# Keys and values of seven tile pairs by seven half-size products for eight, weights through the piece ring

## The chip, the cores and the metric

The kernel runs on one core of one Trainium2 chip. The metric is the device time of one execution in microseconds; lower is better. The core has five engines with queues of their own: TensorE (PE, with its weight loads listed as PEld), VectorE (DVE), ScalarE (ACT), GpSimd (POOL) and SyncE (SP), which here issues all transfers. All data is float32.

## The reference

An attention layer and a LoRA mixture-of-experts layer, each between layer norms and with a residual sum, on 4 sequences of 512 tokens of 1024 features:

```python
# attention: 32 query heads, 8 key/value heads, 32 features each
qkv = x @ w_qkv.T + b_qkv
q, k, v = jnp.split(qkv, [q_dim, q_dim + kv_dim], axis=-1)
...
q = apply_rope(q, 0)
k = apply_rope(k, 0)
...
scores = jnp.einsum('bhqd,bhkd->bhqk', q, k) / math.sqrt(HEAD_DIM)
scores = jnp.where(causal[None, None, :, :], scores, jnp.float32(-1e+20))
attn = jax.nn.softmax(scores, axis=-1)
...
return out @ w_o.T + b_o

# mixture of experts: 8 experts of rank 16, the best 2 of each token
gate_logits = jnp.einsum('bsd,ed->bse', x, gate_w)
...
result = jnp.einsum('bsd,od->bso', x, base_w) + base_b
...
return result + SCALING * lora_out

# around them
x = x + _layernorm(attention(_layernorm(x)))
x = x + _layernorm(experts(_layernorm(x)))
```

The change concerns the product that gives keys and values: 1024 input features by 512 outputs (256 of keys, 256 of values) for every token.

## The kernel before

**Tiles.** The 2048 tokens are 16 tiles of 128, four to a sequence. A tile is loaded (`load_x`, tile `xa`, one buffer), normed and transposed into `xnT` (`normed_x`; two buffers, named `T_xn` in the profile). From it come keys and values (`keys_values`) and queries (`queries`), then attention in groups of heads (`scores`, `turn`, `values`, giving `aT`), the output product (`attention_out`, `acc_o`), norms, the gate (`gated`, `acc_gl`) and the base product of the experts (`ffn`, `acc_f`).

**Products.** A plain product of a tile by 512 columns of weights is eight products of 128 features, summed in one PSUM bank (`project`, L618). `whole` does that with plain weights. `seven` computes a 2 by 2 block product, two tiles by the two halves of the 1024 outputs, with the features also in two halves, by seven half-depth block products for eight (Strassen's method in Winograd's form): each block is four products of 128 features by 512 columns. It needs four sums and differences of the two tiles' transposed inputs (`s1` to `s4`, tag `part`, four buffers in `part_slots`) and, for four of the seven blocks, sums and differences of the weights' quarters. Each block's bank is added by DVE onto earlier ones (`take`, L727), and two combinations of results follow at the blocks 4 and 5 (`combine`, L343, on DVE or POOL, whichever the planner finds sooner). Queries, output and base products of tile pairs go through `seven`; only the first pair's queries and the last pair's output do not.

**Mixed weights.** The sums of weights are made once by `mix`: for a chunk it loads two tiles of 128 rows by 1024 columns (L423, 512 KB each, `wide` tiles, four buffers in `w_slots`), combines their halves in four steps on DVE or POOL and stores both back to DRAM as `mixed_q`, `mixed_o` or `mixed_f` (L438). Two chains run side by side, each with two chunks of q and then two of o; when both are done (`has_w`), four chunks of f follow one by one. `attended` gives the first pair's output tiles (`w`, also `wide`) only after `has_w`.

**The piece ring.** The weights of `whole` and `seven` are streamed in pieces of 128 by 512 (256 KB) by `bring_pieces` (L489), in the order in which the main lane uses them, through a ring of 13 buffers. A piece of a mixed weight waits for its chunk. All transfers stand in SyncE's one queue, in order.

**Keys and values before.** `w_qkv`'s 512 key/value columns are loaded into SBUF at the start (`wkv_sb`, eight transfers of 256 KB, 16 KB of each partition) and stay there. For each tile `keys_values` does eight products of 512 columns (`acc_kv`), then DVE adds the bias to the values (L938) and the keys (L948), the keys are turned (`rotate`) and transposed (`turn_k`).

**The order.** `Order` is a planner that runs while the program is built. It holds costs of every operation (`Op`, `Step`), tracks which buffers and data are free and due, and writes each engine's instructions out in the order in which it would start them. For TensorE it has lanes: scores first, then transposes, values, and the dense lanes `gl_lane`, `kv_lane` and `main_lane`, of which the first with a ready step is taken, a started accumulation going on first. The main lane's own order is fixed: queries of pair 0 and 1; then for each pair n its output, the queries of pair n+2 and its base products. The last pairs' blocks are interleaved by hand. A sequence's last tile comes before its first in the last sequence (tokens 13, 14, 15, 12), so the pairs 6 and 7 of the attention are (13, 14) and (15, 12), while keys and values are made in the order of the tokens, and tile 12's input is normed a second time for its queries (`T_xn_12q`).

Of the kernel before, what the change touches and what calls it, by code (L numbers as in the profile page):

```python
# [11 lines left out]
F32 = mybir.dt.float32  # L12
# [4 lines left out]
P = 128  # L17
# [248 lines left out]
def kernel(  # L266
# [27 lines left out]
    BANKS, SOFT, RING = 4, 8, 13  # L294
# [44 lines left out]
    def combine(urgent, out, in0, in1, op, engines=("dve", "pool")):  # L339


        def issue(engine):
            engine.tensor_tensor(out=out(), in0=in0(), in1=in1(), op=op)  # L343

        on = {"dve": (0.85, partial(issue, nc.vector)), "pool": (1.3, partial(issue, nc.gpsimd))}
        return Op(urgent, **{e: on[e] for e in engines})
# [21 lines left out]
    wkv_sb = const.tile([P, ND, 2 * KVD], F32, name="wkv_sb")  # L368
# [15 lines left out]
    def loads(what):  # L384
# [13 lines left out]
    plain = {"q": w_qkv, "o": w_o, "f": w_base}  # L398
    mixed = {name: dram.tile([D, D], F32, name=f"mixed_{name}") for name in plain}
    has_mixed = {(name, c): Task() for name in plain for c in range(ND // 2)}  # L400
    biases = {
        "q": bqkv_sb,
# [3 lines left out]
    bias_steps = {name: const.tile([P, 512], F32, name=f"bias_step_{name}") for name in plain}  # L406
    has_bias = {name: Task() for name in plain}

    def mix(chunks):

        lo, hi = slice(0, 512), slice(512, D)
        for name, c in chunks:
            w = plain[name]
            a_rows, b_rows = (slice((k + c) * P, (k + c + 1) * P) for k in (0, ND // 2))
            pair = []
            for rows in (a_rows, b_rows):
                yield w_slots.take()

                def bring():
# [3 lines left out]
                    nc.sync.dma_start(out=pair[-1], in_=w[rows, :D])  # L423

                yield sp(P * D * 4 / 1024 / RATE, bring, 1)
            yield LANDS
            a, b = pair
            for out, in0, in1 in (
# [5 lines left out]
                yield combine(2, lambda: out, lambda: in0, lambda: in1, ALU.subtract)  # L434
            for rows, t in ((a_rows, a), (b_rows, b)):
                yield sp(
                    P * D * 4 / 1024 / RATE,
                    lambda: nc.sync.dma_start(out=mixed[name][rows, :], in_=t),  # L438
# [7 lines left out]
    def bias_step(name):  # L446
        yield loaded["b", name]
        b = biases[name]
        yield combine(
            4, lambda: bias_steps[name], lambda: b[:, 512:D], lambda: b[:, :512], ALU.subtract  # L450
# [16 lines left out]
    def block(name, of, h, k, uses=1):  # L467

        new = []
        for c in range(ND // 2):  # L470
            at = (h * ND // 2 + c) * P
            after = has_mixed[name, c] if of is mixed else Task(0.0)
            new.append(Piece(of[name][at : at + P, k * 512 : (k + 1) * 512], after, uses))
        return new

    def bring_pieces():
# [5 lines left out]
        pieces = dict.fromkeys(step.piece for step in main_lane if step.piece is not None)  # L482
        for k, piece in enumerate(list(pieces)):
            yield piece.after
            yield piece_slots.take()

            def issue():
                piece.sb = weights.tile([P, 512], F32, tag="piece", name=f"piece_{k}")
# [119 lines left out]
    def project(lhsT, w, n, name, needs, take):  # L608
# [15 lines left out]
        for c in range(len(needs)):  # L624
            us = 0.858 if n == 512 else 0.24
# [1128 lines left out]
```

## Time and profile before

| | |
|---|---|
| runs | 1163.82 us median of 3 (1163.1 to 1165.35) |
| the profiled execution | span 1162.7 us from first to last instruction; granted clock 0.996 in the mean |
| key/value products, `acc_kv` L618 | 256 matmuls for 128 products, 119.4 us busy, median 592 ns of one |
| additions behind them, L938 and L948 | 16 each of 128x256 on DVE, 418 and 402 ns |
| product with 136 columns, `acc_gl` | 256 matmuls, 34.0 us busy, mean 280 ns |
| `combine` on 128x512, L343 | 859 ns on DVE (`w<-w,w`), 1309 ns on POOL (`y<-y,w`) |
| weight load of a product | 190 ns, on PEld beside the matmuls |
| mixing transfers | q: 512 KB, 6.6 us to landing; back 7.3 us |
| tile transfers | `xa` 256 KB, 3.8 us to landing; output 256 KB, 3.9 us |
| all DMA | 231.48 MB, mean 199 GB/s |

A float32 product appears as two matmuls and two weight loads. Matmuls are pipelined: one lasts longer than the distance to the next, so the length of a run of them, less one duration, divided by one less than their number gives the spacing. The page's time from issue to landing is a median.

### The profile page before, as it was taken

Reading aid. Unit: us, or ns where it says so; the run is one execution under the profiler, and the core shown is the slowest. Engines: PE = TensorE matmul, PEld = TensorE weight load, DVE = VectorE, ACT = ScalarE, POOL = GpSimd, SP = SyncE. Lnnn points to the kernel's source line nnn. Section 1 sums busy time; section 2 is a strip of 40 time slices with the busy share of each in tenths; the row PEclk is TensorE's granted clock in tenths of the full one; section 3 lists DMA queues with packets and bytes.
Section 4 is the critical chain, followed back from the end, with each engine's and each line's share of the span. In section 5 each row is a group of like instructions: output and inputs, shape, how many; then the busy total and the mean of one; then the engine's idle time right before and its main releaser. Section 6 shows DMA issues by size and latency. Waiting matters only on the chain.

```text
span 1162.7 us, 21371 instructions
## 1 busy us (share of the span) xinstructions
PE 1136.4 (98%) x7240; PEld 624.5 (54%) x7240; DVE 832.6 (72%) x1629; ACT 530.1 (46%) x1545; POOL 611.7 (53%) x859
## 2 busy tenths in 40 slices
PE   7999999999999999999999999999999999999997
PEld 3455554655556455565555555456555555556443
DVE  4787767987678756787667876768866787668564
ACT  0354554555555355555434434455644555454010
POOL 2686856743756435544555253654545564547231
PEclk9999999999999999999999999999999999999999
DMA  9879777563773637625477443673457745585783
GB/s 349 277 255 310 248 253 263 170 220 97 257 239 96 199 109 253 192 83 176 141 244 256 137 135 118 219 229 106 149 168 233 243 135 160 164 268 187 221 285 118
DMA packets 117740, 231.48 MB, mean 199 GB/s; under 512 B 13440, under 2 KB 14464, under 8 KB 117632
## 3 DMA queue, kind: packets, MB, share of 16 engines
q1 hardware_dynamic: 117632, 230.12, 60.7%
q8 instruction: 58, 0.95, 0.3%
q14 instruction: 50, 0.41, 0.1%
HBM read 209.09 MB, written 20.97 MB: 198 GB/s over the span
## 4 chain that ended last, share of the span: by engine, by line
PE 86%; DVE 7%; DMA 3%; POOL 1%; ACT 1%; issue 1%; SPq 0%; POOLq 0%; ACTq 0%
PE acc_f L618 18%; PE acc_o L618 16%; PE acc_q L618 14%; PE pt_p L1485 11%; PE acc_kv L618 8%; PE sc L1390 7%; PE av L1508 6%; PE acc_gl L618 2%; DVE nmax L1469 2%; PE pt_xn L593 1%; PE pt_h L593 1%; DMA piece<-in_w_qkv_dram 1%; ACT pr L1411 1%; PE pt_q L1010 1%; DMA xa<-in_x_dram 1%
## 5 line engine op out<-in xcount | busy, mean ns | idle before, releaser
L1425 POOL TENSOR_SCALAR pr<-pr,rtot 128x256 f32<-128x256 f32 (+3 forms) x512 | 300.5, 602 | 251.9 <-DVE rtot L1440 183.3
L1411 ACT ACTIVATE pr<-sc,nmax 128x256 f32<-128x256 f32 (+3 forms) x512 | 265.0, 536 | 121.8 <-DVE nmax L1469 63.6
L1469 DVE TENSOR_REDUCE nmax<-sc 128x2 f32<-128x768 f32 (+3 forms) x176 | 198.2, 1126 | 33.7 <-ACT pr L1411 30.6
L1485 PEld LDWEIGHTS pt_p<-ident,pr 128*128 128x128 f32 x1280 | 144.5, 141 | 59.3 <-issue 49.1
L1485 PE MATMUL pt_p<-ident,pr 128*128 128x128 f32 x1280 | 173.2, 276 | 2.4 <-DVE raw_q L727 1.0
L335 ACT COPY prT<-pt_p 128x512 f32<-128x512 f32 (+1 forms) x261 | 134.1, 548 | 62.4 <-PE pt_p L1485 61.0
L1459 DVE TENSOR_TENSOR sc<-sc,cmask 128x256 f32<-128x256 f32 (+2 forms) x176 | 96.7, 550 | 48.6 <-PE sc L1390 39.0
L335 ACT COPY aT<-av 128x128 f32<-128x128 f32 (+2 forms) x83 | 26.1, 315 | 222.1 <-PE av L1508 222.0
L618 PE MATMUL acc_f<-piece,s_f 128*128 128x512 f32 x256 | 120.1, 602 | 2.1 <-DVE s_f L343 2.1
L618 PE MATMUL acc_kv<-wkv_sb,T_xn 128*128 128x512 f32 x256 | 119.4, 597 | 0.0
L1411 ACT ACTIVATION_READ_ACCUMULATOR pr<-sc,nmax 128x1 f32 x512 | 108.3, 212 | 0.0
L618 PE MATMUL acc_o<-piece,aT 128*128 128x512 f32 x232 | 105.9, 594 | 0.0
L618 PE MATMUL acc_q<-piece,s_q 128*128 128x512 f32 x224 | 105.4, 595 | 0.1
L618 PE MATMUL acc_q<-piece,T_xn 128*128 128x512 f32 x224 | 103.9, 594 | 0.1
L618 PE MATMUL acc_o<-piece,s_o 128*128 128x512 f32 x224 | 102.8, 593 | 0.0
L1390 PE MATMUL sc<-kT,qT 32*128 32x384 f32 (+3 forms) x1024 | 93.9, 464 | 0.5 <-ACT pr L1411 0.5
L1508 PEld LDWEIGHTS av<-prT,v 128*32 128x32 f32 x2560 | 64.8, 109 | 50.1 <-issue 35.0
L618 PE MATMUL acc_f<-piece,T_h 128*128 128x512 f32 x192 | 90.0, 592 | 0.0
L343 POOL TENSOR_TENSOR y<-y,w 128x512 f32<-128x512 f32 x61 | 79.1, 1309 | 20.3 <-ACT w L568 14.9
L1508 PE MATMUL av<-prT,v 128*32 128x128 f32 x2560 | 88.7, 276 | 0.2 <-DVE prT L336 0.2
L336 DVE COPY prT<-pt_p 128x512 f32<-128x512 f32 (+1 forms) x91 | 58.3, 642 | 31.3 <-PE pt_p L1485 29.7
L541 POOL TENSOR_TENSOR rstd<-veps,neg_half 128x1 f32<-128x1 f32 x64 | 35.0, 549 | 86.1 <-DVE veps L537 85.8
(154 smaller groups left out, 1416.3 us busy)
## 6 DMA issues: line engine op xcount, KB each, us to landing
piece<-mixed_f SPq DMA_DIRECT2D x128, 256.0 KB, 3.5
piece<-in_w_o_dram SPq DMA_DIRECT2D x116, 256.0 KB, 3.6
piece<-mixed_q SPq DMA_DIRECT2D x112, 256.0 KB, 3.4
piece<-mixed_o SPq DMA_DIRECT2D x112, 256.0 KB, 4.1
piece<-in_w_qkv_dram SPq DMA_DIRECT2D x100, 256.0 KB, 3.7
piece<-in_w_base_dram SPq DMA_DIRECT2D x96, 256.0 KB, 3.3
xa<-in_x_dram SPq DMA_DIRECT2D x32, 256.0 KB, 3.8
y<-in_x_dram SPq DMA_DIRECT2D x16, 512.0 KB, 5.7
```

Source lines behind the costliest of these rows:

```text
L335: act=(0.15 + n * 0.00085, lambda: nc.scalar.copy(out(), in_())),
L336: dve=(0.15 + n * 0.00105, lambda: nc.vector.tensor_copy(out(), in_())),
L343: engine.tensor_tensor(out=out(), in0=in0(), in1=in1(), op=op)
L541: nc.gpsimd.tensor_tensor(out=self.rstd, in0=self.veps, in1=neg_half, op=ALU.pow)
L618: nc.tensor.matmul(acc[0][:, :n], lhsT=lhsT(c), rhs=w(c), start=(c == 0), stop=last)
L1390: nc.tensor.matmul(sc[:, r, c * n : (c + 1) * n], lhsT=tok.qT[g.kt][rows, (g.at + c) % GROUP, :], rhs=seq.kT[g.kt][rows, :n], start=True, ...
L1411: lambda: nc.scalar.activation(pr[:, c * n : (c + 1) * n], sc4[:, r, c, :], AF.Exp, bias=nmax[:, r, c : c + 1], accum_out=total[:, r, c : ...
L1425: lambda: nc.gpsimd.tensor_scalar(pr[:, c * n : (c + 1) * n], pr[:, c * n : (c + 1) * n], rtot[:, r, c : c + 1], 1.0, ALU.mult, ALU.mult,),
L1459: lambda: nc.vector.tensor_tensor(out=diag, in0=diag, in1=cmask.unsqueeze(1).unsqueeze(1).to_broadcast([P, q, g.n, P]), op=ALU.add,),
L1469: lambda: nc.vector.tensor_reduce(nmax[:, some, : g.n], sc4[:, some], AX.X, ALU.max, negate=True),
L1485: nc.tensor.transpose(pt[:, j, :], g.pr[r][:, j * P : (j + 1) * P], ident)
L1508: nc.tensor.matmul(av[r * HD : (r + 1) * HD, c, :], lhsT=g.seq.v[j][:, head * HD : (head + 1) * HD], rhs=g.prT[r][:, c * (i + 1) + j, :], ...
```

## The change

Keys and values of the first two tiles are still made by `keys_values`, eight products each, now with pieces of the ring that both tiles use. Those of the other fourteen tiles are made in pairs (2, 3), (4, 5) to (14, 15) by `seven`, with the keys' 256 columns and the values' 256 columns as the two halves. Each block is four products of 256 columns.

- `wkv_sb` is gone. The ring has 20 buffers for 13. A key/value piece is still 256 KB: two chunks of 128 rows by 256 columns side by side (`block`, `weight`).
- `mix` makes a fourth set, `mixed_kv`, of 1024 rows by 512 columns: four chunks at half the width, in the same two chains, ahead of q and o.
- The sums of a pair's inputs are a class of their own (`Sums`). For pairs 1 to 5 keys/values and queries share one set, which is held until both have used it; for pairs 6 and 7, where the tiles differ, each has its own. The inputs' tiles are given back only when the sums are made (`freed`).
- `bring_pieces` follows `piece_line`: the pieces of keys and values of pair n+2 stand behind the output pieces of pair n and ahead of the queries of pair n+2. The steps themselves stay in `kv_lane`.
- A key/value block ends with an addition of 256 columns on DVE; two combinations of 256 columns follow in each pair. `combine` and the planner's costs take the width into account.
- The bias and the rope table are loaded behind the first eight pieces (`has_first`), as they were behind the eight loads of `wkv_sb`.

```diff
-    BANKS, SOFT, RING = 4, 8, 13
+    BANKS, SOFT, RING = 4, 8, 20
...
-    wkv_sb = const.tile([P, ND, 2 * KVD], F32, name="wkv_sb")
...
-    plain = {"q": w_qkv, "o": w_o, "f": w_base}
-    mixed = {name: dram.tile([D, D], F32, name=f"mixed_{name}") for name in plain}
+    plain = {"kv": w_qkv[:, D:], "q": w_qkv[:, :D], "o": w_o, "f": w_base}
+
+    width = {name: 256 if name == "kv" else 512 for name in plain}
+    mixed = {
+        name: dram.tile([D, 2 * width[name]], F32, name=f"mixed_{name}") for name in plain
+    }
...
+        n = width[name]
+        rows = 512 // n
         new = []
-        for c in range(ND // 2):
+        for c in range(0, ND // 2, rows):
             at = (h * ND // 2 + c) * P
-            after = has_mixed[name, c] if of is mixed else Task(0.0)
-            new.append(Piece(of[name][at : at + P, k * 512 : (k + 1) * 512], after, uses))
+            after = Task(0.0)
+            if of is mixed:
+                after = [has_mixed[name, c + m] for m in range(rows)]
+            in_ = of[name][at : at + rows * P, k * n : (k + 1) * n]
+            piece = Piece(in_.rearrange("(c p) n -> p c n", p=P), after, uses * rows)
+            new += [(piece, m) for m in range(rows)]
         return new
...
-        pieces = dict.fromkeys(step.piece for step in main_lane if step.piece is not None)
+        pieces = dict.fromkeys(step.piece for step in piece_line if step.piece is not None)
         for k, piece in enumerate(list(pieces)):
+            if k == ND:
+                has_first.finish(order.at)
             yield piece.after
             yield piece_slots.take()
...
+        def used(self, k):
+            self.left[k] -= 1
+            if not self.left[k]:
+                yield [self.has[m] for m in ((2,), (4,), (), ())[k - 1]]
+                part_slots.give(order.at)
...
+        def freed(k):
+            yield sums.taken
+            free(k, order.at)
+
...
+    def keys_values_of_two(pair, sums):
...
+        def out(k, h):
+            tok = toks[k]
+            if h:
+                return (seq.v[tok.i] if tok.i in seq.v else new_v(tok))[:, :]
+            if k not in raw:
+                raw[k] = new_raw(f"k_{tok.t}")
+            return raw[k][:, :KVD]
...
+        steps = seven(
+            "kv",
+            f"{toks[0].t}",
+            sums,
+            out,
+            [has_room],
+            ended,
+            lambda k, at: pair[k].read(at),
+        )
...
             mixes = [
-                start(mix([(name, k + 2 * c) for name in ("q", "o") for c in range(half)]), order.at)
+                start(
+                    mix([(name, k + 2 * c) for name in ("kv", "q", "o") for c in range(half)]),
+                    order.at,
+                )
                 for k in range(2)
             ]
...
+    def kv_of(pair, uses):
+        sums = Sums(f"kv_{pair[0].name}", [j.xnT for j in pair], [j.ready for j in pair], uses)
+        turns, products = keys_values_of_two(pair, sums)
         turn_lanes.extend(turns)
-        main_lane.extend(products)
+        kv_lane.extend(products)
+        piece_line.extend(products)
+        return sums
...
+    def qkv_of(n):
+        at = 2 * n
+        if n < len(pairs) - 2:
+            q_of(pairs[n], kv_of(jobs[at : at + 2], 2))
+        elif n == len(pairs) - 2:
+            kv_of(jobs[at : at + 2], 1)
+            q_of(pairs[n])
+            kv_of(jobs[at + 2 : at + 4], 1)
+        else:
+            q_of(pairs[n])
...
-    q_of(pairs[1])
+    qkv_of(1)
     for n, pair in enumerate(pairs[:-2]):
         out_of(pair)
         if n + 2 < len(pairs):
-            q_of(pairs[n + 2])
+            qkv_of(n + 2)
         ffn_of(pair)
```

## The prediction

> **What bounds the kernel now.** I read the page first: the busy times, the 40 slices, then the chain that ended last.
>
> ```profile
> span 1162.7 us, 21371 instructions
> ...
> PE 1136.4 (98%) x7240; PEld 624.5 (54%) x7240; DVE 832.6 (72%) x1629; ACT 530.1 (46%) x1545; POOL 611.7 (53%) x859
> ...
> PE 86%; DVE 7%; DMA 3%; POOL 1%; ACT 1%; issue 1%; SPq 0%; POOLq 0%; ACTq 0%
> ```
>
> TensorE is busy for 1136.4 of 1162.7 us and holds 86% of the chain; no other engine is above 72%. So the time is TensorE's work plus its 26.3 us of gaps, and a change counts by what it does to either. Next the busy times by stretch, to see where the gaps lie and where DMA is short (columns: length, busy PE, PEld, DVE, ACT, POOL, granted clock, DMA share, GB/s).
>
> ```profile
> 0.00:27.00 27.00, 19.58 (x54) 9.82 (x55) 11.53 (x25) 1.87 (x2) 6.53 (x18) 1.00 0.97 346
> 27.00:60.00 33.00, 32.64 (x133) 16.19 (x131) 22.84 (x42) 11.39 (x41) 20.95 (x30) 1.00 0.85 291
> 60.00:84.00 24.00, 23.49 (x149) 12.84 (x149) 20.48 (x32) 12.47 (x47) 19.86 (x28) 1.00 0.68 233
> 84.00:110.00 26.00, 26.00 (x182) 15.07 (x181) 18.73 (x35) 14.52 (x50) 15.26 (x23) 1.00 0.96 336
> ...
> 200.00:1100.00 900.00, 895.73 (x5978) 499.64 (x5977) 659.09 (x1308) 436.74 (x1262) 466.34 (x661) 1.00 0.57 181
> ```
>
> From 200 to 1100 us only 4.3 us are idle, and DMA is at 0.57. The first 150 us are another regime: DMA at 0.68 to 0.97, TensorE still full. What fills it there, and what the fill waits for, is in two timelines: TensorE's, and SyncE's queue.
>
> ```profile
> 140.23 2.74 PE L618 MATMUL acc_kv<-wkv_sb,T_xn 128*128 128x512 f32 x6
> ...
> 144.19 0.93 PE L1390 MATMUL sc<-kT,qT 32*128 32x384 f32 x8
> 145.05 0.86 PE L1508 MATMUL av<-prT,v 128*32 128x128 f32 x24
> 145.84 1.53 PE L1485 MATMUL pt_p<-ident,pr 128*128 128x128 f32 x12
> 147.21 3.60 PE L618 MATMUL acc_o<-piece,aT 128*128 128x512 f32 x8
> ...
> 211.89 1.32 PE L618 MATMUL acc_gl<-wgl_sb,T_h 128*128 128x136 f32 x10
> ...
> 1128.77 5.40 PE L618 MATMUL acc_f<-piece,s_f 128*128 128x512 f32 x8 [2.10 <-DVE s_f L343]
> ```
> ```profile
> 27.65 2.29 SPq L423 DMA_DIRECT2D mix_q<-in_w_qkv_dram  x3
> ...
> 50.04 0.32 SPq L489 DMA_DIRECT2D piece<-mixed_q  x1
> 50.45 0.39 SPq L423 DMA_DIRECT2D mix_q<-in_w_qkv_dram  x1
> ...
> 72.98 0.32 SPq L489 DMA_DIRECT2D piece<-mixed_q  x1
> ...
> 82.08 0.32 SPq L489 DMA_DIRECT2D piece<-mixed_q  x1
> ...
> 138.28 0.32 SPq L489 DMA_DIRECT2D piece<-mixed_o  x1
> ```
> ```profile
> SPq L489 <- DMA mixed_q<-mix_q: 27.3, 4, 7.5
> ```
>
> The reader is to see that the first chunk of mixed query weights takes 22.4 us from its load (27.65) to the moment a piece can be read back (50.04), the next chunk of that chain 22.5 us (50.45 to 72.98), and that the fourth is there only at 82.08. The last mixed output weight is there at 138.28. SyncE stands still 27.3 us behind four of these stores. TensorE's first s_q product starts at 84.0 and the first output product at 147.2, directly behind mixing; both times it was kept busy by key/value products that need only weights already in SBUF.
>
> **Products removed.** A float32 product is two matmuls. Eight in a row take 3.60 us: seven spacings and one duration of 0.592 (acc_kv's median), so a spacing of 0.429. Ten of 136 columns (acc_gl, mean 0.280) take 1.32 us, so 0.115. The line through both gives 0.215 us at 256 columns; half of 0.429 is 0.2145, twice 0.115 is 0.230. I take 0.215. Seven pairs lose 7 x 16 products of 2 x 0.429 = 96.1 us and get 7 x 28 of 2 x 0.215 = 84.3: **-11.8 us** (-5.9 at 0.230, -12.0 at best).
>
> **Vector work added.** Removed are 28 additions of 256 columns; added are 49 such, 14 half-width combinations inside kv, eight sums (pairs 6 and 7 need a set for kv and another for q, the other five share), 16 half-width combinations in mixing and one bias step. At 0.42 us for an addition (v row), 0.86 or 1.3 for 512 columns on DVE or POOL and half of that for 256, this is 8.8 + 14 x 0.43 to 0.65 + 8 x 0.86 to 1.3 + 17 x 0.43 to 0.65, 29 to 39 us. From 200 to 1100 DVE idles 241 us and POOL 434, which hides it: nothing. Uncovered, it shows as a missing PSUM bank: a block of four products now lasts 1.72 us, and an addition behind one 1.22 us nmax needs 1.64, which fits; behind two it needs 2.86, 1.1 late, and once in each pair that is 8 us. Bounds 0 and +8; I take 0, by the idle time.
>
> **Transfers added.** 98 pieces of 256 KB (25.7 MB) and 16 mixing transfers of 256 KB (4.2 MB); the eight first weight loads stay as pieces. Every issue takes 0.33 us of SyncE. Behind 200 us a pair adds 14 pieces per some 140 us, 26 GB/s on 181, where the first stretch moved 346: nothing. The deeper ring can win at most the 4.3 us of gaps, so this stage is bounded by -4 and +8, and I take 0.
> The Trainium skill, DMA: Bandwidth & Descriptors, section Bandwidth, says to batch transfers to 1 MiB or more for 75% of its peak of 435 GB/s, against streaming 256 KB at a time. The first stretch, mostly such transfers, moved 346 GB/s, 80% of that, so the row overrules it; by the rule, estimated at half of the peak (218 GB/s), the 207 GB/s needed later would be at the edge and the term would be near its upper bound.
>
> **The start, where the change costs.** Mixing now goes kv, q, o in the same two chains with the same four wide tiles, so two kv chunks stand ahead of the first q chunk in each. A kv chunk: load 3.8 us (x tiles of 256 KB) for 6.6, store 3.9 (output tiles) for 7.3, the remaining 8.5 of the 22.4 halved to 4.3: 12.0 us, two of them 24. The kv fetches also put their waits into SyncE's queue, with the next mix loads behind them. Against that, the first o chunk was combined by 88.7 and stored only at 100.0, held behind the fetches for pair 1's queries; late queries take this hold away, 11.3 us. So the first output product moves by 24 - 11.3 = **13 us** (bounds 0, if DMA's free share hides all of it, and 24).
> The fill is gone too. By 147.2 TensorE had done key/value products of six tiles, 41.2 us. Now it can do tiles 0 and 1 (13.7) and pair 1 (12.0); pair 2's pieces stand in the ring's order behind all 28 output pieces of pair 0, and those wait for mixing. That is **15.4 us** of work not done by the same point. Attention may fill some: a group gives 0.93 + 0.86 + 1.53 = 3.3 us of TensorE in some 9.2, 0.36 of 13 us, 4.7 (bounds 0 and 4.7; I take 4.7, as the planner takes any ready lane). Idle added: 13 + 15.4 - 4.7 = **23.7 us** (15.4 to 39.4).
> Part of it is paid again in the clock: behind the 2.10 us gap at 1128.77, eight matmuls took 5.40 us for 3.60. Once: **+1.8** (0 to 5.4, three times).
> The Trainium skill, TensorE: Matmul & The Clock Gate, Part 1, puts the fall to half clock behind an idle window of some 3.4 us; here 2.1 us was enough. By the page short waits cost nothing and the term is 0; by the row it is the 1.8.
>
> What is late next: the f weights, mixed from 141.0 to 240.1 and first needed at 254.9. They start 13 us later, but so does their user, and kv of pair 2 (12.0) before it replaces one tile (6.9), so their 14 us of room stays. Pair 1's last scores were 33 us ahead of its output (271.3, 304.0). Nothing more is added.
>
> **Sum:** -11.8 + 23.7 + 1.8 = +13.7; 1162.7 becomes 1176.4. The runs' median is 1163.8, 1.1 above this span, so **1177 us**.
>
> **Rivals.** *Mixing catches up (the other side):* if the output products start 15 us earlier than before, at 132, nothing is lost and the products' gain stands: 1163.8 - 11.8 = 1152, with up to 4 us of later waits 1154. It wins from a start before 143.6 (15.4 - 11.8 = 3.6 ahead of 147.2). For it: SyncE's 27.3 us and a DMA share of 0.68 are room in the chain. Against it: 7.9 MB more by then (mixing 4.2, pair 1's pieces 3.7), 23 us at 346 GB/s. *Only the fill is lost:* mixing ends as before, 15.4 - 11.8 = +3.6, **1167**. For it the same room, against it the chunks in series. *Evictions rule kv:* the start as forecast and the 8 us of late banks, with three clock falls instead of one: 1177 + 8 + 3.6 = **1189**; for it DVE's 85% from 60 to 84 us, against it 27% free later. *Halving that does not halve:* if weight loads (190 ns) set the spacing, 256 columns would gain less; but 136 columns go at 115 ns with the same loads, so this gets no chance of its own.
>
> **How the numbers follow.** Forecast 0.62 (own range 1167 to 1197: from -12.0 + 15.4 to -11.8 + 39.4 + 5.4, on 1163.8), catches up 0.17, only the fill 0.13, evictions 0.08. A measurement of this kernel can't tell 0.2% (2.3 us) from no change. Slower: 0.62 + 0.08 + 0.08 of the third case = 0.78; the same 0.05, from that case's lower edge; faster 0.17. The range 1160 to 1196 leaves out most of the faster case (0.15) and a little at the top.
>
> **What would show it.** Right: kv matmuls of 256 columns 0.215 apart; TensorE busy about 1125 us but with idle tenths between 80 and 165 us, ended by pieces from mixed weights; the first s_q product of pair 1 past 100, the first output product near 160; SyncE waiting longer on mixed stores. Wrong: no such gap, or output products before 144; or gaps behind DVE evictions of kv all along.

## The result, and the profile after

The changed kernel takes 1222.31 us (median of 4 runs, 1221.43 to 1225.82) against 1164.59 for the kernel before beside it: ratio 1.0505, 95% interval 1.0488 to 1.0522. The forecast was 1177, with 1196 as its upper end. The first lines of the changed kernel's page:

```profile
span 1221.0 us, 21984 instructions
...
PE 1156.7 (95%) x7408; PEld 671.5 (55%) x7408; DVE 850.7 (70%) x1665; ACT 533.3 (44%) x1541; POOL 644.1 (53%) x887
...
PE   7987877999999999999999999999999999999997
...
PEclk9988877999999999999999999999999999999999
...
PE 81%; DVE 9%; POOL 4%; ACT 2%; DMA 2%; issue 1%; POOLq 0%; SPq 0%; ACTq 0%; DVEq 0%
```

Two things grew together. TensorE idles 64.3 us instead of 26.3, and it is also busier, 1156.7 instead of 1136.4, although its products became cheaper. Both lie in slices three to seven. The busy times of the changed kernel by stretch show it (columns as in the prediction):

```profile
27.00:60.00 33.00, 33.00 (x159) 16.89 (x157) 21.77 (x40) 9.11 (x39) 17.12 (x28) 1.00 0.61 213
60.00:84.00 24.00, 18.49 (x128) 15.25 (x125) 18.58 (x31) 12.55 (x53) 15.96 (x31) 0.86 0.70 240
84.00:110.00 26.00, 22.81 (x222) 15.55 (x220) 19.43 (x38) 14.88 (x48) 20.06 (x31) 0.93 0.61 228
110.00:150.00 40.00, 28.84 (x137) 14.24 (x137) 17.15 (x28) 8.35 (x24) 15.43 (x17) 0.79 0.67 233
150.00:200.00 50.00, 36.17 (x259) 21.37 (x258) 34.72 (x66) 24.88 (x69) 36.09 (x39) 0.76 0.50 190
200.00:1100.00 900.00, 887.76 (x6000) 521.39 (x5997) 654.65 (x1279) 436.02 (x1240) 488.45 (x663) 1.00 0.65 213
```

Before, the same view had for two of these stretches:

```profile
110.00:150.00 40.00, 38.05 (x288) 22.13 (x287) 31.81 (x61) 21.38 (x67) 31.31 (x38) 1.00 0.71 242
150.00:200.00 50.00, 48.73 (x331) 25.18 (x330) 36.17 (x69) 24.64 (x74) 33.59 (x43) 1.00 0.81 261
```

From 60 to 200 us TensorE is idle for 33.7 us (3.7 before) and its granted clock is 0.76 to 0.93 (1.00 before), while DMA is at 0.50 to 0.70: it isn't DMA's rate that is missing. SyncE's timeline names what is (the mixing transfers, and the piece fetches between them):

```profile
31.25 2.10 SPq L432 DMA_DIRECT2D mix_kv<-in_w_qkv_dram  x4
...
59.53 4.43 SPq L447 DMA_DIRECT2D mixed_kv<-mix_kv  x4
...
74.48 2.25 SPq L511 DMA_DIRECT2D piece<-mixed_kv  x4
76.78 3.22 SPq L511 DMA_DIRECT2D piece<-in_w_qkv_dram  x4
80.42 2.57 SPq L432 DMA_DIRECT2D mix_q<-in_w_qkv_dram  x4
...
126.05 1.12 SPq L432 DMA_DIRECT2D mix_o<-in_w_o_dram  x1
...
141.72 3.47 SPq L511 DMA_DIRECT2D piece<-mixed_q  x7
145.63 3.60 SPq L511 DMA_DIRECT2D piece<-in_w_o_dram  x4
150.03 1.80 SPq L432 DMA_DIRECT2D mix_o<-in_w_o_dram  x3
...
201.30 1.82 SPq L511 DMA_DIRECT2D piece<-mixed_o  x2
```

Mixing of the query weights begins at 80.42, where before it began at 27.65. The 52.8 us between are 3.6 of a later begin, 32.7 for the key/value chunks (31.25 to 63.96, when their last stores are out) and 16.5 in which 15 fetches of pieces and two input tiles, with SyncE's waits for them, go ahead of the next loads. At 126.05 one tile of an output chunk is loaded, and its other tile and the second chunk follow only at 150.03, with 25 piece fetches and two input tiles between. Of the four chunks of mixed output weights the third and fourth are fetched in the last line, the fourth at 202.8; before, the fourth was fetched at 138.28, 64.5 us earlier.

On TensorE's timeline this is a row of waits and slow work (in brackets the idle time before the line and what ended it):

```profile
69.29 1.09 PE L1113 MATMUL pt_q<-ident,raw_q 128*128 128x128 f32 x4 [5.06 <-DVE rtot L1540]
...
109.34 1.02 PE L640 MATMUL acc_q<-piece,s_kv 128*128 128x512 f32 x2
...
115.94 0.69 PE L1585 MATMUL pt_p<-ident,pr 128*128 128x128 f32 x2 [3.51 <-POOL pr L1525]
...
130.03 2.07 PE L640 MATMUL acc_q<-piece,s_kv 128*128 128x512 f32 x2 [4.58 <-DMA piece<-mixed_q]
...
208.90 1.97 PE L640 MATMUL acc_o<-piece,aT 128*128 128x512 f32 x2
```

Pair 1's first query products with mixed weights, its second block, begin at 109.34 (84.0 before). Half-way through they wait 4.58 us for a mixed piece, and two of their matmuls then take 2.07 us for 1.02. The first output product is at 208.90, 61.7 us later than before. But of the 35.0 us of gaps between 60 and 210 us only 5.1 are ended by a mixed piece; 27.6 are ended by steps of the softmax (`pr`, `rtot`). By these rows TensorE stood still mostly because no product was at hand while a group of attention was not ready.

To compare kernels I split each profiled span in three: the time of the key/value matmuls, that of all other matmuls (each counted from the end of the matmul before it to its own end), and TensorE's idle time. "Early" is the idle time ahead of the first output product, "late" that from 200 to 1100 us.

| kernel | span | kv matmuls | other matmuls | idle | early | late | first output product |
|---|---|---|---|---|---|---|---|
| before | 1162.7 | 111.6 | 1024.8 | 26.3 | 10.2 | 4.3 | 147.2 |
| changed | 1221.0 | 102.4 | 1054.3 | 64.3 | 43.3 | 12.2 | 208.9 |
| e5_mix_first | 1177.2 | 100.1 | 1032.8 | 44.3 | 24.3 | 9.4 | 147.0 |
| f1_before_unmixed | 1156.5 | 112.0 | 1021.2 | 23.3 | 7.4 | 4.6 | 128.7 |
| f2_after_unmixed | 1159.4 | 100.2 | 1026.7 | 32.5 | 10.8 | 9.1 | 119.7 |
| g1_resident3 | 1161.4 | 103.7 | 1029.0 | 28.7 | 13.3 | 4.6 | 149.6 |
| g2_resident4 | 1161.0 | 106.3 | 1026.0 | 28.7 | 15.1 | 3.2 | 150.9 |

The change costs 58.3 us of span: -9.2 in its own matmuls, +29.5 in all others, of which there are as many as before, and +38.0 idle.

### The profile page after: what moved, and what is told of

It is laid out like the page before. It is cut to its first block, busy times and chain, and to the rows that moved or that the text cites. A ratio compares the mean times of both kernels' runs of the same rounds, so it can differ in the third digit from the quotient of the medians.

```text
span 1221.0 us, 21984 instructions
## 1 busy us (share of the span) xinstructions
PE 1156.7 (95%) x7408; PEld 671.5 (55%) x7408; DVE 850.7 (70%) x1665; ACT 533.3 (44%) x1541; POOL 644.1 (53%) x887
## 4 chain that ended last, share of the span: by engine, by line
PE 81%; DVE 9%; POOL 4%; ACT 2%; DMA 2%; issue 1%; POOLq 0%; SPq 0%; ACTq 0%; DVEq 0%
PE acc_f L640 17%; PE acc_o L640 15%; PE acc_q L640 13%; PE pt_p L1585 11%; PE acc_kv L640 7%; PE sc L1490 7%; PE av L1608 5%; DVE nmax L1569 3%; PE acc_gl L640 2%; POOL pr L1525 2%; ACT pr L1511 2%; DVE sc L1559 1%; PE pt_h L615 1%; PE pt_q L1113 1%; PE pt_xn L615 1%
## 5 line engine op out<-in xcount | busy, mean ns | idle before, releaser
L1525 POOL TENSOR_SCALAR pr<-pr,rtot 128x256 f32<-128x256 f32 (+3 forms) x512 | 304.6, 612 | 211.4 <-DVE rtot L1540 163.4
L1585 PE MATMUL pt_p<-ident,pr 128*128 128x128 f32 x1280 | 181.4, 285 | 14.4 <-POOL pr L1525 11.6
L1585 PEld LDWEIGHTS pt_p<-ident,pr 128*128 128x128 f32 x1280 | 150.7, 146 | 69.5 <-issue 39.4
L335 ACT COPY prT<-pt_p 128x512 f32<-128x512 f32 (+1 forms) x250 | 128.7, 548 | 110.5 <-PE pt_p L1585 109.5
L1490 PE MATMUL sc<-kT,qT 32*128 32x384 f32 (+3 forms) x1024 | 97.9, 481 | 9.0 <-ACT pr L1511 9.0
L335 ACT COPY aT<-av 128x128 f32<-128x128 f32 (+2 forms) x76 | 23.6, 310 | 178.9 <-PE av L1608 178.9
L336 DVE COPY prT<-pt_p 128x512 f32<-128x512 f32 (+1 forms) x102 | 65.3, 643 | 48.4 <-PE pt_p L1585 47.3
L1608 PE MATMUL av<-prT,v 128*32 128x128 f32 x2560 | 96.8, 282 | 2.0 <-DVE prT L336 0.9
L1608 PEld LDWEIGHTS av<-prT,v 128*32 128x32 f32 x2560 | 68.1, 111 | 55.0 <-issue 31.8
L343 POOL TENSOR_TENSOR y<-y,w 128x512 f32<-128x512 f32 x61 | 79.0, 1312 | 16.8 <-DVE w L584 11.3
L640 PE MATMUL acc_q<-piece,s_kv 128*128 128x512 f32 x160 | 77.8, 610 | 5.5 <-DMA piece<-mixed_q 5.1
L1490 PEld LDWEIGHTS sc<-kT,qT 32*128 32x128 f32 x1024 | 40.9, 190 | 66.6 <-issue 29.9
```

The costliest lines, as they stand in the source:

```text
L335: act=(0.15 + n * 0.00085, lambda: nc.scalar.copy(out(), in_())),
L336: dve=(0.15 + n * 0.00105, lambda: nc.vector.tensor_copy(out(), in_())),
L640: nc.tensor.matmul(acc[0][:, :n], lhsT=lhsT(c), rhs=w(c), start=(c == 0), stop=last)
L1490: nc.tensor.matmul(sc[:, r, c * n : (c + 1) * n], lhsT=tok.qT[g.kt][rows, (g.at + c) % GROUP, :], rhs=seq.kT[g.kt][rows, :n], start=True, ...
L1525: lambda: nc.gpsimd.tensor_scalar(pr[:, c * n : (c + 1) * n], pr[:, c * n : (c + 1) * n], rtot[:, r, c : c + 1], 1.0, ALU.mult, ALU.mult,),
L1585: nc.tensor.transpose(pt[:, j, :], g.pr[r][:, j * P : (j + 1) * P], ident)
```

## The experiments

The theory: the loss is made by the order in which SyncE's one queue issues piece fetches and mixing transfers, which holds the query and output weights back. The rivals: the mixing of keys and values costs its time whatever the order; the lost fill of the start; the narrow blocks with their additions. In all tables that follow, "first" is the start of the first output product (147.2 before, 208.9 in the changed kernel).

**One part at a time.**

```diff
# e1_kv_unmixed (changed kernel; key/value blocks read plain quarters, kv isn't mixed)
+            of = plain if name == "kv" else of
-                    mix([(name, k + 2 * c) for name in ("kv", "q", "o") for c in range(half)]),
+                    mix([(name, k + 2 * c) for name in ("q", "o") for c in range(half)]),
# e2_before_kv_mix (before; kv chunks are mixed ahead of q and o, and nobody reads them)
-                start(mix([(name, k + 2 * c) for name in ("q", "o") for c in range(half)]), order.at)
+                start(mix([(name, k + 2 * c) for name in ("kv", "q", "o") for c in range(half)]), order.at)
...
# e3_before_no_fill (before; keys and values of tiles 4 and 5 wait for the end of mixing)
-        needs[0] += [has_raw]
+        needs[0] += [has_raw] + [has_w] * (t in (4, 5))
# e4_three_plain (changed; pairs 0 to 2 by eight plain products, kv mixed behind f)
-            yield start(mix([("f", c) for c in range(2 * half)]), order.at)
+            yield start(mix([(m, c) for m in ("f", "kv") for c in range(2 * half)]), order.at)
...
```

> The changed kernel with the four kv chunks of mixing left out: the key/value blocks that should read mixed weights read plain quarters of the same size, so keys and values are not the reference's; number, size and order of products, pieces, evictions and sums stay. Theory Q (the kv chunks stand ahead of q and o in the mixing chains and everything behind them is late): the first output product returns from 208.9 to 145-157 us, and the time to 1160-1175 (1163.8 - 11.8 + 15.4 for the fill that is still lost = 1167). Rival V (the narrow kv blocks, their evictions, the shared sums and the kv pieces in the ring cost all along): 1200 or more. Between 1175 and 1200 both have a part.

> The kernel before, with only the changed kernel's four kv chunks of mixing added ahead of q and o, into a DRAM tensor that nobody reads; products, ring and fill as before. Theory Q: the first output product moves from 147 to 180-205 us, TensorE idles 15-35 us more before it and runs at half clock in part of it, time 1190-1215 (the changed kernel's 1222 less the 15 us of fill, plus the 11.8 of products not saved). Rival V: under 1175, since kv's products are as before.

> The kernel before, with the key/value products of tiles 4 and 5 held back until all q and o chunks are mixed, nothing else. It prices the fill alone, in the forecast 13.7 us of products (two tiles of 6.86). If the fill counts as forecast: 1172-1182, the first output product still near 147-162 us with the two tiles' products behind the end of mixing. Rival (attention takes their place): under 1168.

> The changed kernel with keys and values of the first three pairs by eight plain products from pieces of the ring (so tiles 4 and 5 fill the start again), the other five pairs by seven, and the kv chunks mixed last, behind f. Theory Q: the start is as before, five pairs save 1.7 us each, 8.4 together: 1152-1160 and faster than before. Rival V: five sevenths of the changed kernel's loss stay, 1195 or more; 1175 or more if half of it is V's.

| run | median us | ratio, 95% interval | first |
|---|---|---|---|
| e1_kv_unmixed | 1182.6 | 1.0161, 1.0141 to 1.0181 | 172.7 |
| e2_before_kv_mix | 1195.2 | 1.0269, 1.0247 to 1.0292 | 188.2 |
| e3_before_no_fill | 1181.9 | 1.0155, 1.0134 to 1.0175 | 172.9 |
| e4_three_plain | 1203.5 | 1.0338, 1.032 to 1.0355 | 169.8 |

Each part is dear by itself, and the parts overlap: they don't add up to the loss. Without the key/value mixing the changed kernel is 39.7 us faster; the same mixing in front of the kernel before makes that one 31.9 us slower, and its first output product 41 later, where the forecast for the changed kernel had 13. e1 still misses its theory (1160 to 1175, output product at 145 to 157): it lies between theory and rival, and its output product stands where e3's does. Holding back two tiles of fill, with nothing else changed, costs 18.6. Of e3's 17.7 us of span 10.7 are idle time ahead of the first output product (20.9 against 10.2) and 7.1 are matmuls that took longer; the forecast had 15.4 less 4.7, also 10.7, as idle time. It also moves the first output product by 25.7, out of the 147 to 162 expected, though no transfer was added: the fill doesn't only occupy TensorE, what the planner puts behind it moves too. e4 keeps the fill and takes the key/value mixing away from the front, and still loses; 1203.5 is its rival's sign, not its theory's. From 200 to 400 us TensorE is busy for only 176.1 us (199.4 before). That is the stretch in which key/value chunks, now behind f, are mixed in the wide tiles that activations need. With tiles of their own (e7c and e7 below) it is busy for 187.2 and 198.0 us there, but these runs changed ring or order too, so what the shared tiles cost was not separated.

**The queue's order alone.**

```diff
# e5_mix_first (changed; mixing loads, and the stores likewise, go ahead of piece fetches)
-                yield sp(P * 2 * n * 4 / 1024 / RATE, bring, 1)
+                yield sp(P * 2 * n * 4 / 1024 / RATE, bring, -1)
# e6_ring13 (changed; the ring as before)
-    BANKS, SOFT, RING = 4, 8, 20
+    BANKS, SOFT, RING = 4, 8, 13
```

> The changed kernel, with mixing's loads and stores taken by the planner ahead of piece fetches in SyncE's queue (urgency -1 for 1), nothing else. Theory P (besides the chunks in front, mixing is late because piece fetches go ahead of it in SyncE's order: the q loads went out at 80.4 us, three of the first o loads at 150, each behind 16 to 18 fetches): q loads by 65-70, first output product at 165-190 for 208.9, time 1180-1205. Rival C (the length of a mixing round itself, DMA and combinations, sets it): 1215-1228, the first output product past 200.

> The changed kernel with the ring put back from 20 to 13 buffers, nothing else. Theory P: fewer fetches can stand ahead of mixing, so it comes earlier, 1195-1212. Rival C: within 6 of 1222. If the ring's depth is needed later (kv's pieces come 14 to a pair on top of the 28 of queries): above 1228, with gaps behind piece transfers between 300 and 1100 us.

e5: 1177.3 us, 1.0118 (1.0093 to 1.0143). e6: 1203.0, 1.0339 (1.0319 to 1.036), first output product at 199.5. With not one transfer or product fewer, the order in SyncE's queue is worth 45 of the 58 us; e5 came out faster than the theory's 1180 to 1205. The same view of e5's SyncE:

```profile
38.99 1.90 SPq L432 DMA_DIRECT2D mix_q<-in_w_qkv_dram  x4
...
84.43 1.92 SPq L432 DMA_DIRECT2D mix_o<-in_w_o_dram  x4
...
128.13 0.91 SPq L511 DMA_DIRECT2D piece<-mixed_o  x2
...
143.61 0.38 SPq L511 DMA_DIRECT2D piece<-mixed_o  x1
```

The query chunks are loaded at 38.99 instead of 80.42, the fourth output chunk is fetched at 143.61 instead of 202.8, and the first output product is at 147.0, where it was before the change, although four more chunks were mixed. The shorter ring alone wins 19, as expected: with 13 slots fewer fetches can be issued ahead of a waiting mixing load.

**Order and tiles together.** These seek the best of both: kv mixed behind f in two half-width tiles of its own with pairs 0 to 2 plain (e7, e7c, e9, e12), two pairs plain (e11), the first pieces ahead of mixing (e8, e9, e10, e11), and mixing begun only when a number of pieces are issued (e12, e13).

```diff
# e7_own_late: e4 with ring 18, urgency -1 for mixing, and
-                yield w_slots.take()
+                yield (kv_slots if name == "kv" else w_slots).take()
# e7c_own_late_ring13: e7 with ring 13 and mixing's urgency as it was
# e8 (before, mixing's urgency -1), e9 (e7), e10 (e5), e11 (e9, two pairs plain): the first 16 (e8) or 24 pieces first
-            yield sp(P * 512 * 4 / 1024 / RATE, issue)
+            yield sp(P * 512 * 4 / 1024 / RATE, issue, -2 if k < 24 else 0)
# e12_own_held (e7), e13_mix_held (e5): has_begun is finished when 18 or 20 pieces are issued
+            yield has_begun
             half = ND // 4
```

> A version meant to beat both: keys and values of the first three pairs plain (the fill is back), the other five pairs by seven; the kv chunks mixed behind f in two half-width tiles of their own, so that they do not wait for the wide tiles (in the run with three plain pairs they were loaded only at 314 us, and TensorE idled 19 us from 300 to 400); mixing's transfers ahead of piece fetches; ring of 18. If the late kv chunks were what that run lost past 300 us, and P holds for its start (first output product at 169.8): 1150-1162. If the ring's order does not matter at the start: 1172-1185. If the narrow blocks cost by themselves: 1185 or more.

> The same version with the ring of 13 and mixing behind piece fetches as in the kernel before. Its start is then the kernel before's, but for kv weights that come as 24 pieces for eight loads. P: 1152-1166, the first output product at 145-158. Under C the same as the version with the ring of 18, to 6 us.

> The kernel before, with mixing ahead of the piece fetches in the queue, save the first 16 pieces: the order alone, without the change. Under P the order is worth something only where mixing is late; before, TensorE idled 4 us between 27 and 150: 1158-1165. If 1155 or less, the order is a gain of its own and the changed kernel's repair must be read against it.

> The version with three plain pairs and late kv chunks in tiles of their own, in the same order of the queue (24 pieces, mixing, the rest). It idled 7.3 us at 36 us for its first pieces when mixing went ahead of them. With five pairs saving 8.4 us and the fill in place: 1153-1166. If 16 more fetches of plain kv weights at the start cost what the fill brings: 1170-1180.

> The changed kernel in this order of SyncE's queue: the first 24 pieces (weights of the first two tiles), then mixing, then all other pieces. With mixing ahead of everything the first output product was back at 147.0, as before the change, but TensorE idled 14 us more before 100 us, for its first pieces. Theory P in full (the order of the queue, not the amount of mixing, is what the changed kernel lost beyond the fill): output product at 147-160, less idle before 100 us, 1165-1176. If what is won at the start comes back as later mixing: 1177-1190.

> The same with two plain pairs: six pairs save 10.1 us, tiles 4 and 5 no longer fill the start, eight fetches fewer. If the fill is worth what holding it back cost (18.6 us): 1170-1178. If a start that is not late needs no fill: 1153-1163.

> Three pairs with plain keys and values as eight products, the keys' and values' mixing behind that of the feed-forward in tiles of its own, ring of 18, and the mixing chains begin only when 18 pieces are issued, then go ahead of further pieces. Theory Q (what was left of the loss in e7, e9 and e10 is the order of the first loads): first output product at 145 to 155 us, 1155 to 1170 us. Rival (the loss is in work that mixing adds to the engines of the start, whatever the order): 1175 us or more.

> The changed kernel with mixing transfers ahead of pieces, as in e5_mix_first, but the chains begin only when 20 pieces are issued. Theory Q: first output product at 147 to 160 us, 1165 to 1177 us. Rival (the loss left in e5 is the work and wait of mixing four weights ahead of the output product, whatever the order): 1177 us or more.

| run | median us | ratio, 95% interval | first |
|---|---|---|---|
| e7_own_late | 1183.4 | 1.017, 1.0153 to 1.0186 | 164.6 |
| e7c_own_late_ring13 | 1181.3 | 1.0151, 1.0134 to 1.0168 | 160.8 |
| e8_before_mix_second | 1177.4 | 1.0114, 1.0099 to 1.013 | 152.7 |
| e9_own_second | 1175.6 | 1.0098, 1.0083 to 1.0113 | 151.4 |
| e10_mix_second | 1180.4 | 1.0142, 1.0125 to 1.0159 | 153.3 |
| e11_two_plain | 1208.0 | 1.0373, 1.0355 to 1.0392 | 139.1 |
| e12_own_held | 1170.8 | 1.006, 1.0045 to 1.0076 | 139.9 |
| e13_mix_held | 1175.0 | 1.0101, 1.0084 to 1.0118 | 144.2 |

None reaches the kernel before, and most missed what the theory expected. e7 and e7c missed 1150 to 1162 and 1152 to 1166; they differ by 2.1 us, within the 6 that were the rival's sign: what mixing first wins later (7.7 us idle against 14.4 from 200 to 1100) it loses ahead of the output product (26.8 against 15.3). e9 and e10 landed in the ranges named for the case that the theory fails, e8 above its 1158 to 1165, e11 above both of its ranges.

e8 is the one that warns: the same reordering on the kernel before costs 13.5 us. Its idle time up to 60 us is 13.6 instead of 7.8 (in e9 15.5, in e10 15.6, in e5 14.7), probably because pieces now pass the loads of bias and rotary table (issued at 14.99 and 15.66 us, before at 6.73 and 8.03). That is about half of the cost; the rest is matmuls that took longer (+6.6). With mixing held back this idle time is 12.0 in e12 and 7.4 in e13. e12 wins 4.8 on e9; e13's 2.2 on e5 lie within the spread of e5's two runs (1175.5 and 1179.0). So the order of the first loads was at most a part of what was left: e12 is just above the theory's 1155 to 1170, and e13 near the upper end of its 1165 to 1177.

e11 starts earliest of these and is the slowest: TensorE idles 22.1 us from 200 to 1100, with four gaps of 3.1 to 4.1 us by 251, while the first mixed weights of keys and values are fetched only from 223 to 253. An early first output product is no gain in itself.

**The products without any mixing.**

```diff
# f1_before_unmixed, f2_after_unmixed (before, changed; every block reads its plain weight)
+            of = plain
...
+            mixes = []
...
```

> The kernel before with the weights' mixing left out for queries, output and feed-forward: every block reads its plain weight, so the output is not the reference's. It gives the base for the next run: the start's waits for mixed weights are gone from both. Both theories expect first output product near 140 to 150 us or earlier, and a time below before, 1140 to 1164 us.

> The changed kernel with the weights' mixing left out for all four: every block reads its plain weight, so the output is not the reference's. Theory P (the change's loss is all in the way mixed weights arrive; seven products for eight is worth about 12 us by itself): 8 to 16 us below the run f1_before_unmixed. Rival V (half-width key and value blocks with their shared sums, evictions and 32 pieces a pair cost by themselves what the products save): not below f1_before_unmixed, 0 to 10 us above it.

f1: 1158.9 us, 0.996 (0.9946 to 0.9975); f2: 1163.6, 0.9996 (0.9987 to 1.0005), both against the same runs of before. My theory expected 8 to 16 us of gain and got a loss of 4.6, inside the rival's 0 to 10. (A pair brings 14 pieces of keys and values, not the 32 that the expectation names.) The stretches behind the start, f1 first:

```profile
60.00:150.00 90.00, 89.25 (x563) 49.96 (x562) 66.76 (x121) 47.77 (x163) 47.38 (x77) 1.00 0.37 118
...
200.00:1100.00 900.00, 895.45 (x5972) 499.32 (x5970) 656.31 (x1298) 434.60 (x1260) 464.64 (x661) 1.00 0.54 176
```
```profile
60.00:150.00 90.00, 84.98 (x611) 54.20 (x609) 64.86 (x118) 50.88 (x165) 51.28 (x84) 0.98 0.56 177
...
200.00:1100.00 900.00, 890.93 (x6091) 522.51 (x6090) 669.11 (x1328) 438.15 (x1262) 471.62 (x663) 1.00 0.61 198
```

By the table of spans, the key/value matmuls fall from 112.0 to 100.2, the -11.8 of the forecast; the other matmuls take 5.5 more and TensorE idles 9.2 more, so the span grows by 2.9. Of the idle time 4.3 us lies from 60 to 150, nearly all in three gaps that attention ends, and 4.5 behind 200, in gaps of less than 1 us with many causes: softmax, the rotation of queries and keys, a sum of inputs. TensorE's timeline of f1, then of f2:

```profile
62.79 6.17 PE L618 MATMUL acc_kv<-wkv_sb,T_xn 128*128 128x512 f32 x14
```
```profile
64.59 1.55 PE L1609 MATMUL av<-prT,v 128*32 128x128 f32 x28 [1.41 <-ACT prT L335]
...
82.11 3.70 PE L640 MATMUL acc_q<-piece,T_xn 128*128 128x512 f32 x8 [1.30 <-DVE prT L336]
...
132.56 1.12 PE L1491 MATMUL sc<-kT,qT 32*128 32x384 f32 x8 [1.85 <-ACT pr L1512]
```

In f2 these are waits for attention of one group while no other product is at hand; where the first of them lies, f1 runs a key/value tile from the weights in SBUF. So the saving is real, and by these rows the same change takes away the work that stood in for it. That the shorter products alone open the gaps, and not f2's 14 fetches for each pair, is argued; DMA ends none of the three.

**Weights kept for the start.** The last two give the start its fill back: kv weights stay in SBUF and serve the first pairs whole, then they are mixed in place, and the remaining pairs go by seven.

```diff
# g1_resident3 (changed; ring 12; wkv_sb and its loads as before; pairs 0 to 2 whole from it)
+    def mix_kv():
+        yield [s.done for s in kv_steps]
+        yield from mix([("kv", c) for c in range(ND // 2)])
...
+            if name == "kv":
+                pair += [wkv_sb[:, c, :], wkv_sb[:, c + ND // 2, :]]
# g2_resident4: the same with pairs 0 to 3 whole
```

> Key/value weights kept in SBUF as before, their products for pairs 0 to 2 as eight whole tiles from them (the fill of the start is back), then mixed in place in SBUF behind the last of these products, stored, and pairs 3 to 7 by seven half-width products with streamed pieces; ring of 12. Theory Q (the products' gain is real at 11.8 us for seven pairs, 8.4 for five, and the whole loss lies in the start): first output product at 145 to 152 us, keys' and values' matmuls 103 to 104 us in all, 1153 to 1160 us, below before. Rival (narrow blocks bring waits of their own behind 200 us that take the gain back): 1163 us or more with TensorE's idle time from 200 to 1100 us at 10 us or more (before 4.3).

> As g1_resident3, but pairs 0 to 3 take whole products from SBUF and only pairs 4 to 7 go by seven (the mixing in place comes later, its pieces too). Theory Q: gain of 6.7 us for four pairs, 1155 to 1161 us. Rival: 1163 us or more.

g1: 1163.3 us, 0.9995 (0.9986 to 1.0005). g2: 1162.0, 0.9988 (0.9979 to 0.9997): the fastest that computes the reference, but by less than the 0.2% that counts here. Both miss the theory's ranges (1153 to 1160 and 1155 to 1161). But the rival's condition isn't met either (late idle 4.6 and 3.2 us, not 10 or more), so narrow blocks with streamed pieces add no idle time behind 200 us here. The key/value matmuls of g1 are as expected, 103.7 (7.9 saved). What took the gain is, in part, again a gap in the fill. g1's stretch and part of its timeline:

```profile
110.00:150.00 40.00, 34.45 (x294) 21.15 (x293) 32.53 (x61) 20.44 (x61) 32.45 (x42) 0.89 0.64 227
```
```profile
138.91 1.66 PE L1492 MATMUL sc<-kT,qT 32*128 32x384 f32 x8 [2.48 <-ACT pr L1513]
140.51 2.82 PE L1587 MATMUL pt_p<-ident,pr 128*128 128x128 f32 x12
...
147.41 0.93 PE L1492 MATMUL sc<-kT,qT 32*128 32x384 f32 x8 [2.12 <-ACT pr L1513]
```

Before, a key/value tile lay from 134.5 to 144.3, just here. In g1 that tile, the sixth, ran from 161.8 to 172.3: as much fill, spent elsewhere. Idle time of 5.6 us instead of 2.0 in this stretch (+2.4 over the whole span) and longer matmuls (+4.2 over the whole span, the granted clock here 0.89) leave 1.3 of the 7.9. That the tile's place makes the gap is argued from these rows.

## Why the prediction was right and wrong

The sign was right, and so was the mechanism in the large: the change loses more at the start than its products win. The size was not; the time is 45 us above the forecast and 26 above its range. By its own steps:

- **Products removed, -11.8:** right. The matmuls of 256 columns are 216 ns apart (median; forecast 215), and f1 against f2 gives -11.8 in all. In the changed kernel itself it is -9.2: there the same matmuls took 102.4 where f2 has 100.2.
- **Vector work added, transfers added, 0 (-4 to +8):** the later idle time grew by 7.9 us in the changed kernel and by 4.5 between f1 and f2, near the upper bound. The cause named for that bound, the additions behind key/value blocks, isn't what the traces show: none of these gaps is ended by one. In the changed kernel 3.9 of the 12.2 us end with the last step of the rotation of queries or keys, 4.5 with softmax or copies of its result, most of the rest with layer norm and gate; and g1 with five narrow pairs has no such loss.
- **The first output product moves by 13 us:** the step that failed. It moved by 61.7. Its two terms were 24 for the kv chunks and -11.3 for a hold that goes. The chunks took 32.7. Their transfers were not the reason (in the median 4.9 us to landing for a load and 2.0 for a store, where 3.8 and 3.9 were forecast), but SyncE waited 16.2 us for their combinations, with four loads and then four stores of both chains together, where before the chains alternated. The hold didn't go, it grew: 16.5 us of fetches ahead of the first query loads, 24 ahead of the output's, and the way from the first query load to the fetch of the fourth output chunk took 122.4 us where it was 110.6. I had read from the trace which piece fetches held a store back, but priced the new order as if the queue went on serving mixing at the old pace; a ring of 20 lets more fetches pass. e5 shows that the order alone brings the output product back to 147.0, e6 that the ring has a part. The number of fetches is not all of it: on that longer way 30 pieces were fetched, before 38.
- **Fill not done, 15.4, less 4.7 for attention:** as idle time it was right where a run prices it alone: e3, with 13.7 us of products held back, idles 10.7 us more. Its other 7.1 us, in longer matmuls, belong to the clock term.
- **Idle added at the start, 23.7 (15.4 to 39.4):** 33.1, inside its bounds (the lower one leaves out the 4.7 of attention; with it, it is 10.7). The 61.7 us of shift cost only that, as products of pair 1 and attention went on. That so large a miss in the shift stays inside the bounds is luck.
- **Clock, +1.8 (0 to 5.4):** the other large miss. I counted falls as single events; the start became a chain of waits. From the stretches shown, 24 x 0.14, 26 x 0.07, 40 x 0.21 and 50 x 0.24 make 25.6 us of full clock lost from 60 to 200, some of it in idle time. By the table all other matmuls took 29.5 us more. The records of the clock give 50.7 us of busy time at half clock, 3.4 before, hence 23.6 lost. In e3, too, they give 11.9 us more, or 6.0 of its 7.1.
- **What is late next, nothing:** true of f's weights: the later idle time is what was named above.

The sum with what was measured is -11.8 + 33.1 + 23.6 and 13.4 left over: 4.9 of idle time behind the first output product, and 8.5 by which matmuls took longer than the clock explains (between f1 and f2 it is 3.8 of their 5.5, as f2's 3.4 us of busy time at half clock cost 1.7), which no run takes apart. Together 58.3. Of the rivals, "Only the fill is lost" asked that mixing end as before. e5 meets that, with the output product at 147.0, and is at 1177, ten above that rival's 1167: its idle time ahead of the output product is 24.3 against 10.2, and its other matmuls take 8.0 us longer. That it lands on the forecast's number is chance. "Mixing catches up" wanted the output product before 143.6; no run with all its mixing in front got there (e13 came to 144.2). "Evictions rule kv" fell with g1 and with the gaps above. Of the signs named in advance, the first s_q product past 100 (109.3) and the idle slices came; TensorE's 1125 us of busy time (1156.7), the output product near 160, gaps ended mostly by mixed pieces and longer waits on mixed stores did not. SyncE waited 3.2 us for the stores of mixed queries (27.3 before), and for the combinations instead:

```profile
SPq L447 <- POOL mix_q L343: 26.5, 6, 10.4
SPq L447 <- DVE mix_o L343: 17.9, 3, 13.5
...
SPq L511 <- DMA mixed_q<-mix_q: 3.2, 4, 1.3
```

The columns are total, number and longest. A wait for stores had become a wait for work that DVE and POOL could only begin once late loads had come, with the softmax of attention in the same queues. That coupling, from late loads to in-order engines to TensorE, is argued from these rows; no run took it apart.

What stays open: why e5 and e13, with the output product back in place, still carry some 5 us more late idle time than before (9.4 and 9.0 against 4.3); and whether g1 would gain its 7.9 us if the planner held the sixth tile back for 134 us, which was not tried.

## What to carry to other kernels

Work that needs nothing is worth more than its length: the resident weights' products were the cover for the waits of the start (13.7 us of them, held back, cost 18.6 in e3), and a change that makes them cheaper but dependent sells the cover. When a change adds transfers to a queue that is served in order, write out the queue anew, with how many other transfers the buffers allow ahead of each; adding the new durations to the old schedule is not enough. And price each new gap of TensorE with the clock that follows it, as often as the gaps repeat.

## What the runs showed of the hardware

The granted clock fell to half behind quite short gaps. Gaps of 1.30, 1.41 and 1.77 us brought no fall (f2 at 80.8 and 63.2, before at 132.2); of two gaps of 1.85 one did (f2 at 130.7) and one did not (e13 at 394.1); gaps of 2.45, 2.48 and 2.88 did (e12 at 301.0, g1 at 136.4, e12 at 47.5), and the fall then lasted 3.4 or 6.8 us. The gap of 2.10 us from which the prediction took its clock term stands near the end of all twenty traces: behind it the clock fell in six of them, the kernel before among these, and not in the other fourteen. So it is not the length alone. In each trace the falls begin whole multiples of 3.41 us apart, as if time were cut into stretches of that length. Counted in such stretches, at full clock, over all traces (without the first 30 and the last 15 us): all 57 with 1.85 us or more of idle TensorE were followed by half clock, 5 of the 26 with 1.5 to 1.85, and 1 of 3998 with less. A gap that lies across two stretches can pass without a fall, and several short ones in one stretch can bring it (e7 near 97 us: four of 0.36 to 0.78 us). In g1 behind the gap of 2.48 us twelve transposes took 2.82 us and eight score matmuls 1.66; behind the next gap, of 2.12, the score matmuls took 0.93 as at full clock, and the fall came with the lines after (four output matmuls 2.99 us, the next four 1.88). The Trainium skill, TensorE: Matmul & The Clock Gate, Part 1, has some 3.4 us as the idle window; here that is how long the shortest falls last, and idle time of a little under 2 us within one stretch was enough. So a gap of some 2 us can, by estimate, cost another 1.7 (half of 3.4) in the work behind it.
